# Two scan layers on one core: LayerNorm by tokens, the gate projection moved, one C product per state pair

## The chip, the cores and the metric

The kernel runs on 1 core of one Trainium2 chip. The metric is device microseconds of one execution; the verdict compares medians of several. The core has five engines with a queue each: PE (TensorE: matmuls, and PEld for their weight loads), DVE (VectorE), ACT (ScalarE), POOL (GpSimd) and SP (SyncE, which only issues DMAs here). An engine does its instructions in program order and waits on semaphores for the others.

## The reference

Two layers of a visual state-space model on `x` [8, 64, 64, 192], float32, each preceded by a normalization over groups of 6 channels and added to its input. One layer, cut to what is computed (K = 2 directions in layer 0, 4 in layer 1; 16 states; 384 inner channels; L = 64 x 64 = 4096 tokens):

```python
xz = jnp.einsum('bhwc,ec->bhwe', x, in_proj_w)          # 192 -> 768
xx, z = jnp.split(xz, 2, axis=-1)                       # 384 each; z is the gate
xc = silu(depthwise_conv_3x3(xx) + conv_b)
xs = ...                                                # the K orders of the 4096 tokens
dts, Bs, Cs = split(einsum('bkdl,kcd->bkcl', xs, x_proj_weight))
delta = softplus(einsum('bkrl,kdr->bkdl', dts, dt_projs_weight) + bias)
def step(h, inp):                                       # over the 4096 tokens
    dA = jnp.exp(dl_t[..., None] * As[None])
    h = dA * h + (dl_t * u_t)[..., None] * B_t[:, :, None, :]
    y = jnp.einsum('bkdn,bkn->bkd', h, C_t)             # the C product and the sum over states
y = sum over directions of (ys + xs * Ds), each put back in row order
y = (y - mean(y)) * rsqrt(var(y) + 1e-5) * ln_w + ln_b  # over the 384 channels of a token
y = y * gelu(z)                                         # silu(z) in layer 1
out = einsum('bhwd,od->bhwo', y, out_proj_w)            # 384 -> 192
```

## The kernel before

Channels lie on the 128 partitions (three tiles `dt` for 384 channels), tokens along the free axis, in chunks of T = 512 tokens, 8 chunks an image. A layer (`vss_layer`) has two stages, one after the other.

**The convolution stage** (`front`) goes over the 8 images in pairs of chunks, 32 pairs. `project` multiplies the normalized input by the first half of the input projection (PE into `pi`) and copies the result into a padded image `pad`. Of the nine taps of the 3 x 3 convolution, `first` does tap 0 on ACT, `second` taps 1 to NV-1 on DVE into `tp`, and `conv` the others on PE, as products with small diagonal blocks (`block_diag`, L151, 32 x 32 each, four at a time side by side); it adds `tp` through `mask` and applies Silu. NV is 5 in layer 0 and 4 in layer 1. The result goes to DRAM, as it is (`xcd`), turned to tokens on partitions (`turn`, `xtd`) and, in layer 1, by image columns (`columns`). `order` writes the order of all this out by hand.

**The scan stage** (`scans`) has a step for each image, direction and chunk: 128 steps in layer 0, 256 in layer 1. A step has 24 slots: 8 pairs of states (`m`) times 3 channel tiles (`dt`). The work of slot g:

- `scan` (L772): two `tensor_tensor_scan` on DVE, one for each state of the pair, h = da * h + hb over 512 tokens; then the product hc = h * C on POOL (L773), 2 x 512 elements a partition, with `cr` a row of C spread over the partitions.
- what `todo` holds for this slot, sorted by `rank_of`.
- `inject` for slot g + 2 (L728): 8 matmuls that put (delta * u) * B into `hb` (two PSUM buffers of two banks).
- `decay` for slot g + 4 (L745): two Exp on ACT into `da` (five buffers).

`at(i, s, f)` puts f into slot s of step i; the tables `L0_SLOTS` and `L1_SLOTS` hold these slots, and slots past 23 run on into the next steps. `reduce` adds hc of a state pair into `py` on PE (24 `block_diag` matmuls, L151), `load_c` loads the next `cr` from the SP queue, `dt_proj`, `dt_bias`, `softplus`, `turn_delta` (L683) and `make_dut` (L691) prepare the next step, `enter` (L665) and `carry` hand the state on. All matmuls of a step other than `hb` and `py` go through one PSUM bank, the tag `m`.

From the last direction of an image on, each finished chunk also goes through the LayerNorm work, functions with f_, spread over 2 steps in layer 0 and 4 in layer 1; the chunks of the last image take one step each (`L0_LAST`, `L1_LAST`), the very last one what remains. In order: `f_norm` normalizes the layer's input again (ACT), `f_gate` projects it to z (PE, 6 matmuls, L871) and `f_keep` copies it out (ACT); `f_sum`, `f_keep_sum` and `f_all` make each token's mean over the partitions by matmuls (L896, L911; `f_mean`, L888, in the last image); `f_center` subtracts it (DVE, L914); `f_square` (ACT), the same sums again, `f_rstd` (Ln and Exp, ACT), `f_scale` (DVE, L925); `f_act` is Gelu or Silu of z (ACT, L930), `f_affine` (ACT, L935), `f_times` (POOL, L944), `f_out` (PE, L950), `f_add` (DVE, L959), `f_store`.

Of the kernel before, what the change touches and what calls it, by code (L numbers as in the profile page):

```python
# [16 lines left out]
B = 8  # L17
# [33 lines left out]
    "turn_b": 3,  # L51
    "keep_b": 4,
    "dt_proj": (7, 0, 4),
    "dt_bias": (8, 2, 5),
    "turn_delta": (12, 15, 14),
    "make_dut": (13, 17, 15),
    "softplus": 10,
    "reduce": (5, 5),
    "add_y": 12,
    "add_turned": 26,  # L60
    "keep_y": 29,
    "f_norm": 8,
    "f_gate": ((9, 10), (18, 18), (22, 22)),
    "f_keep": (11, 20, 23),
    "f_sum": (20, 30),
    "f_keep_sum": (22, 31),
    "f_all": (23, 32),
    "f_center": 24,
    "f_square": 24,
    "f_rstd": 33,  # L70
    "f_scale": 33,
    "f_act": 34,
    "f_affine": (36, 35, 34),
    "f_times": (38, 39, 36),
    "f_out": ((42, 42, 42), (44, 46, 46)),
    "f_add": (43, 47),
# [3 lines left out]
    "load": 6,  # L80
    "f_norm": 8,
    "f_gate": ((10, 10), (11, 11), (9, 9)),
    "f_keep": (11, 12, 10),
    "f_act": 18,
    "f_mean": ((13, 13, 13), (18, 18, 18)),
    "f_center": 14,
    "f_square": 16,
    "f_rstd": 19,
    "f_scale": 19,
    "f_affine": (19, 20, 20),  # L90
    "f_times": (19, 20, 20),
    "f_out": ((21, 22, 22), (26, 26, 26)),
    "f_add": (23, 27),
# [4 lines left out]
    "turn_b": 6,  # L98
    "keep_b": 8,
    "dt_proj": (5, 8, 10),  # L100
    "dt_bias": (6, 10, 11),
    "turn_delta": (14, 15, 13),
    "make_dut": (15, 16, 14),
    "softplus": 11,
    "reduce": (5, 6),
    "add_y": 13,
    "add_turned": 24,
    "keep_y": 29,
    "f_norm": 6,
    "f_gate": ((11, 12), (17, 18), (20, 22)),  # L110
    "f_keep": (13, 19, 24),
    "f_sum": (41, 67),
    "f_keep_sum": (43, 70),
    "f_all": (45, 70),
    "f_center": 48,
    "f_square": 48,
    "f_rstd": 72,
    "f_scale": 72,
    "f_act": 59,
    "f_affine": (72, 76, 72),  # L120
    "f_times": (76, 79, 72),
    "f_out": ((83, 84, 84), (89, 91, 94)),
    "f_add": (85, 95),
}
L1_LAST = {
    "load": 6,
    "f_norm": 18,
    "f_gate": ((20, 20), (19, 19), (21, 21)),
    "f_keep": (21, 20, 22),
    "f_act": 22,  # L130
    "f_mean": ((11, 12, 12), (16, 16, 16)),
    "f_center": 13,
    "f_square": 16,
    "f_rstd": 17,
    "f_scale": 18,
    "f_affine": (19, 19, 19),
    "f_times": (22, 22, 22),
    "f_out": ((24, 24, 24), (28, 28, 28)),
    "f_add": (25, 29),
}  # L140
# [20 lines left out]
def load_weights(tc, ctx, name, w, K, rank, R, mask):  # L161
# [10 lines left out]
    get("w_in", [CP, CT, D], w["in_proj"][:, D:].rearrange("(t p) e -> p t e", p=CP))  # L172
# [27 lines left out]
    t["gnb"] = wp.tile([P, B, 2 + CT], F32, name="gnb")  # L200
    t["grs"] = wp.tile([P, B, 2 + CT], F32, name="grs")
# [3 lines left out]
def front(tc, name, x_src, xcd, xcd_col, xtd, xdd, w_in, t, clear, consts):  # L205
# [4 lines left out]
    ident, mask, grp, mean_w, all_w, eps_gn, eps_ln = consts  # L210
    cw, cb = t["cw"], t["cb"]

    NV = 4 if xdd is None else 5
    NH = NCH // 2
    with tc.tile_pool(name=f"{name}_a1", bufs=1) as a1, tc.tile_pool(
# [3 lines left out]
        w_x1 = a1.tile([P, D], F32, name="w_x1")  # L219
        nc.sync.dma_start(out=w_x1, in_=w_in[:P])  # L220
        w_x2 = a1.tile([P, D], F32, name="w_x2")
# [34 lines left out]
        def spread(im, w, src):  # L256

            for o in range(2 + CT):
# [15 lines left out]
        def group_means(b):  # L274
            im = ims[b]
            im["pg"] = psa.tile([P, 2, 2 + CT], F32, name="pg")
            spread(im, 0, im["mv"][:, :, 0])

        def deviations(b):
            im = ims[b]  # L280
            mv = im["mv"]
            gm = im["gm"] = a2.tile([P, 2 + CT], F32, name="gm")
            nc.vector.tensor_copy(gm, im["pg"][:, 0])
            dv = im["dv"] = a2.tile([P, 2], F32, name="dv")
            nc.vector.tensor_sub(dv, mv[:, :, 0], gm[:, :2])
# [3 lines left out]
        def variances(b):  # L289
            im = ims[b]  # L290
            spread(im, 1, im["dv"])
            gsd = a2.tile([P, 2 + CT], F32, name="gsd")
# [23 lines left out]
        def project(b, p, dt):  # L316
# [3 lines left out]
            cols = slice(dt * P, (dt + 1) * P)  # L320
# [4 lines left out]
            for r in range(2):  # L325
# [8 lines left out]
                )  # L334
            for r in range(2):
                c = 2 * p + r
                copy = nc.scalar.copy if dt == 2 and xdd is not None else nc.vector.tensor_copy
# [3 lines left out]
                )  # L341

# [72 lines left out]
        def order():  # L415
# [7 lines left out]
            for dt in range(DT):  # L423
                project(0, 0, dt)
                first(0, 0, dt)
                second(0, 0, dt)
            first(0, 1, *range(DT))
            second(0, 1, 0)
            normalize(0, 1, 2, 3)
            if B > 1:  # L430
                load(1, 0, 1)
# [5 lines left out]
            for g in range(B * NH):  # L437
# [3 lines left out]
                go = g + 1 < B * NH  # L441
                conv(b, 2 * p)
                for dt in range(DT):
                    if go:
                        project(n, q, dt)
                    if prev:
                        turn(*prev, dt)
                    if go:
                        first(n, 2 * q, dt)
                    if prev and xcd_col is not None:  # L450
                        columns(prev[0], prev[1] // 2, dt)
                    if p == 2 and more and dt == 1:
                        group_means(b + 1)
                if p == 0 and more:
                    load(b + 1, 2, 3)
                second(b, 2 * p + 1, 1, 2)
# [747 lines left out]
```

## Time and profile before

| | us |
|---|---|
| median of 3 runs | 25216.62 (25214.65 to 25219.68) |
| span of the profiled execution | 25231.1 |
| first scan of layer 0, last of layer 1 begin | 961.3, 25182.1 |
| busy in the span: PE, PEld | 24024.7, 13528.4 |
| busy in the span: DVE, ACT, POOL | 23345.8, 19452.6, 22144.2 |

One execution is profiled, and its own span is what sums are made against. In the profile, a line of a group gives the line of the kernel, the engine, the operation, the tiles written and read, their shapes and the number of instructions; then the time that the group kept its engine busy, the mean length of one in ns, and the idle time of the engine just before its instructions with what ended it. Instructions that follow one another overlap, so busy time by number is less than the mean length. PE's records count each float32 matmul twice, each transpose once. 0 to 961 us is the convolution stage of layer 0, then its scans to some 8930, the convolution stage of layer 1 to some 9865, and its scans to the end. The chain of work that ended last lies by 50% on PE, 25% on DVE and 19% on ACT:

```profile
PE 50%; DVE 25%; ACT 19%; issue 5%; DMA 1%; POOL 0%; SPq 0%; DVEq 0%; ACTq 0%; POOLq 0%
DVE h L772 22%; PE hb L728 20%; PE py L151 14%; ACT da L745 8%; PE pt L616 3%; PE pd L568 2%; PE pc L151 2%; PE po L950 2%; PE pz L871 2%; ACT delta L144 2%; ACT L144 1%; ACT L640 1%; PE pi L322 1%; ACT da L753 1%; ACT delta L630 1%
```

### The profile page before, as it was taken

Reading aid. Unit: us, or ns where it says so; the run is one execution under the profiler, and the core shown is the slowest. Engines: PE = TensorE matmul, PEld = TensorE weight load, DVE = VectorE, ACT = ScalarE, POOL = GpSimd, SP = SyncE. Lnnn points to the kernel's source line nnn. Section 1 sums busy time; section 2 is a strip of 40 time slices with the busy share of each in tenths; the row PEclk is TensorE's granted clock in tenths of the full one; section 3 lists DMA queues with packets and bytes.
Section 4 is the critical chain, followed back from the end, with each engine's and each line's share of the span. In section 5 each row is a group of like instructions: output and inputs, shape, how many; then the busy total and the mean of one; then the engine's idle time right before and its main releaser. Section 6 shows DMA issues by size and latency. Waiting matters only on the chain.

```text
span 25231.1 us, 794569 instructions
## 1 busy us (share of the span) xinstructions
PE 24024.7 (95%) x340032; PEld 13528.4 (54%) x340032; DVE 23345.8 (93%) x22142; ACT 19452.6 (77%) x37140; POOL 22144.2 (88%) x10287
## 2 busy tenths in 40 slices
PE   9999999999999999999999999999999999999999
PEld 4555555555555544555555555555555555555554
DVE  7899999999999777999999999999999999999998
ACT  5677788778878767777777777777777777777777
POOL 0499999999999713999999999999999999999998
PEclk9999999999999999999999999999999999999999
DMA  4566666666666555675675575675675575576575
GB/s 161 154 158 158 158 158 159 156 158 159 160 158 159 138 179 195 170 164 168 170 166 168 170 165 169 169 165 169 170 163 170 170 164 169 170 163 171 167 166 143
DMA packets 3836413, 4141.15 MB, mean 164 GB/s; under 512 B 2140460, under 2 KB 2340804, under 8 KB 3829828
## 3 DMA queue, kind: packets, MB, share of 16 engines
q1 hardware_dynamic: 3821296, 4032.72, 61.7%
q8 instruction: 2693, 44.12, 0.8%
q10 hardware_dynamic: 11604, 57.59, 0.6%
q14 instruction: 820, 6.72, 0.1%
HBM read 3443.63 MB, written 645.99 MB: 162 GB/s over the span
## 4 chain that ended last, share of the span: by engine, by line
PE 50%; DVE 25%; ACT 19%; issue 5%; DMA 1%; POOL 0%; SPq 0%; DVEq 0%; ACTq 0%; POOLq 0%
DVE h L772 22%; PE hb L728 20%; PE py L151 14%; ACT da L745 8%; PE pt L616 3%; PE pd L568 2%; PE pc L151 2%; PE po L950 2%; PE pz L871 2%; ACT delta L144 2%; ACT L144 1%; ACT L640 1%; PE pi L322 1%; ACT da L753 1%; ACT delta L630 1%
## 5 line engine op out<-in xcount | busy, mean ns | idle before, releaser
L773 POOL TENSOR_TENSOR hc<-h,cr 128x1024 f32<-128x1024 f32 x9216 | 21566.7, 2368 | 2985.7 <-DMA xt_k<-xtd 1844.7
L772 DVE TENSOR_TENSOR_SCAN h<-da,hb 128x512 f32<-128x512 f32 x18432 | 20860.2, 1199 | 1262.2 <-PE hb L728 1038.8
L745 ACT ACTIVATE da<-delta,a_neg 128x512 f32<-128x512 f32 x18432 | 12249.7, 713 | 1763.7 <-DVE h L772 1736.3
L728 PEld LDWEIGHTS hb<-dg,dut 64*128 64x128 f32 x147456 | 9215.4, 185 | 6720.3 <-issue 5785.3
L728 PE MATMUL hb<-dg,dut 64*128 64x128 f32 x147456 | 10835.6, 286 | 603.9 <-DVE h L772 413.0
L151 PE MATMUL py<-hc,mask 32*32 32x512 f32 x147456 | 6866.8, 601 | 36.0 <-ACT y L821 32.7
L151 PEld LDWEIGHTS py<-hc,mask 32*32 32x32 f32 x147456 | 1582.8, 103 | 2359.7 <-issue 1722.2
L753 ACT COPY da<-a 128x2 f32<-128x2 f32 x8064 | 1562.5, 194 | 293.9 <-ACT da L745 1.8
L778 ACT COPY st<-h 128x6 f32<-128x6 f32 x2688 | 537.4, 200 | 1142.3 <-DVE h L772 1140.0
L616 PE MATMUL pt<-xdbl,w_dt 96*128 96x512 f32 (+1 forms) x2304 | 1302.2, 646 | 38.8 <-DVE yc L914 15.9
L630 ACT ACTIVATE delta<-pt,dtb 128x512 f32<-128x512 f32 x1152 | 787.2, 683 | 449.5 <-PE pt L616 444.4
L355 DVE SCALAR_TENSOR_TENSOR tp<-pad,cw,tp 128x512 f32<-128x512 f32 x1344 | 988.2, 750 | 113.0 <-ACT tp L349 78.9
L683 PE MATMUL pq<-ident,delta 128*128 128x128 f32 x4608 | 758.7, 287 | 324.4 <-DVE dut L691 226.6
L871 PE MATMUL pz<-xn_sq,w_in 96*128 96x512 f32 x1536 | 835.3, 643 | 42.0 <-ACT g L882 27.2
L691 DVE TENSOR_TENSOR dut<-pq,xt_k 128x512 f32<-128x512 f32 x1152 | 767.7, 666 | 83.4 <-PE pq L683 83.4
L568 PE MATMUL pd<-x_k,w_x 128*128 128x512 f32 x1536 | 798.3, 629 | 35.8 <-DVE yc L914 15.1
L950 PE MATMUL po<-yc,w_out 128*96 128x512 f32 x1536 | 783.0, 621 | 16.2 <-POOL yc L944 13.3
L683 PEld LDWEIGHTS pq<-ident,delta 128*128 128x128 f32 x4608 | 484.2, 141 | 522.0 <-DVE dut L691 342.9
L151 PE MATMUL pc<-pad,taps 32*32 32x512 f32 x13824 | 577.9, 592 | 17.1 <-ACT xo L370 13.4
L821 ACT COPY y<-py 128x1536 f32<-128x1536 f32 x384 | 551.7, 1437 | 35.7 <-PE py L151 19.4
L144 ACT ACTIVATE delta<-delta 128x1536 f32<-128x1536 f32 x384 | 570.4, 1485 | 4.3
L944 POOL TENSOR_TENSOR yc<-yc,g 128x512 f32<-128x512 f32 x384 | 490.0, 1279 | 79.1 <-ACT yc L935 72.9
(105 smaller groups left out, 10143.1 us busy)
## 6 DMA issues: line engine op xcount, KB each, us to landing
cr<-cscr SPq DMA_DIRECT2D x2048, 512.0 KB, 4.4
dg<-dgd SPq DMA_DIRECT2D x1536, 512.0 KB, 7.9
cr<-xdd SPq DMA_DIRECT2D x1024, 512.0 KB, 6.4
xt_k<-xtd SPq DMA_DIRECT2D x768, 384.0 KB, 7.1
xcd<-xo SPq DMA_DIRECT2D x128, 768.0 KB, 3.5
xtd<-xv SPq DMA_DIRECT2D x128, 768.0 KB, 4.4
y<-yrow SPq DMA_DIRECT2D x128, 768.0 KB, 5.0
yc<-yrow SPq DMA_DIRECT2D x128, 768.0 KB, 7.2
```

Source lines behind the costliest of these rows:

```text
L144: nc.scalar.activation(out, in_, AF.Softplus)
L151: nc.tensor.matmul(out[j * Q : (j + 1) * Q, dt], w[i * Q : (i + 1) * Q], x[i * Q : (i + 1) * Q], start=first, stop=last, tile_position=(i ...
L568: nc.tensor.matmul(live[i]["pd"][:R], w_x[:, dt, k, :], live[i]["x"][:, dt], start=(dt == 0), stop=(dt == DT - 1),)
L616: nc.tensor.matmul(pt, w_dt[:, k, dt * P : (dt + 1) * P], live[i]["xdbl"][:rank], start=True, stop=True,)
L683: nc.tensor.transpose(pq[:, g], live[i]["delta"][:, dt, g * P : (g + 1) * P], ident)
L728: nc.tensor.matmul(hv[:, r, q], live[i]["dut"][r * G : (r + 1) * G, dt, q], dg[r * G : (r + 1) * G, q, :, 2 * mm : 2 * mm + 2], start=True ...
L745: nc.scalar.activation(da[:, n].rearrange("p (r g j) -> p r g j", r=2, j=G), live[i]["delta"][:, dt].rearrange("p (g r j) -> p r g j", r=2 ...
L753: nc.scalar.copy(da[:, :, f], live[i]["a0"][:, dt, 2 * m : 2 * m + 2])
L772: nc.vector.tensor_tensor_scan(o, a, v, init, ALU.mult, ALU.add)
L773: nc.gpsimd.tensor_mul(hc[:, dt], h[:, dt], live[i]["cr", m])
L871: nc.tensor.matmul(fin["pz"], w_in[:, u, dt * P : (dt + 1) * P], fin["xn"][:, u], start=(u == 0), stop=(u == CT - 1),)
L950: nc.tensor.matmul(fin["po"][:CP], w_out[:, dt, u * CP : (u + 1) * CP], fin["y"][:, dt], start=(dt == 0), stop=(dt == DT - 1),)
```

## The change

Three parts, with new slot tables for all of the scan stage's work.

- The gate projection moves into the convolution stage: `gates` multiplies the same input by the second half of the projection (whose channels stand in the order of the scans), applies Silu in layer 1 (Gelu of layer 0 stays where it was, `f_act`) and stores `zd` in DRAM, from where `f_load_g` fetches it. `f_norm`, `f_gate` and `f_keep` go.
- Taps 1 to NV-1 on DVE become more: NV is 8 in layer 0 and 7 in layer 1. `second` goes over taps and, within each, over the three tiles, and `order` is rewritten.
- LayerNorm works on tokens: `f_turn` transposes 128 tokens x 384 channels through PSUM (PE), and then mean, square sum and scaling are per partition, on ACT, with sums taken by the instructions themselves (`accum_out`); `f_back` transposes back, and `f_affine` reads that from PSUM. Only a 128 x 4 product (`f_rstd`) is DVE's.
- `scan` issues one POOL product for a state pair, after its third tile, with C broadcast over the tiles; `h` has three buffers. The slot of `reduce` moves from 5, 5 to 7, 7 in layer 0 and from 5, 6 to 6, 7 in layer 1.

```diff
-    "reduce": (5, 5),
-    "add_y": 12,
+    "reduce": (7, 7),
+    "add_y": 15,
...
+    "load": (16, 14, 7),
+    "f_act": 39,
+    "f_turn": (18, 20, 21, 22),
+    "f_take": (19, 21, 22, 23),
+    "f_mean": 23,
+    "f_square": (23, 25, 24, 25),
+    "f_rstd": 27,
+    "f_scale": (28, 31, 30, 30),
+    "f_back": (33, 35, 36),
+    "f_affine": (34, 36, 37),
+    "f_times": (39, 39, 39),
...
-    NV = 4 if xdd is None else 5
+    NV = 7 if xdd is None else 8
...
+        def gates(b, p, dt):
+
+            pi = product(b, p, DT + dt)
+            zo = a2.tile([P, 2, T], F32, name="zo")
+            for r in range(2):
+                if gate is None:
+                    nc.scalar.copy(zo[:, r], pi[r])
+                else:
+                    nc.scalar.activation(zo[:, r], pi[r], gate)
+            nc.sync.dma_start(
+                out=zd[b][dt * P : (dt + 1) * P, 2 * p * T : 2 * (p + 1) * T],
+                in_=zo.rearrange("p r l -> p (r l)"),
+            )
...
-        def second(b, c, *dts):
-            for dt in dts:
-                tv = ims[b]["tp", c][:, dt].rearrange("p (h w) -> p h w", w=W)
-                for s in range(1, NV):
+        def second(b, c, *taps):
+            for s in taps:
+                for dt in range(DT) if s < NV else ():
+                    tv = ims[b]["tp", c][:, dt].rearrange("p (h w) -> p h w", w=W)
...
-                    s2.tile([P, DT, 2, T], F32, name="h"),
+                    s2.tile([P, DT, 2, T], F32, name="h", bufs=3),
                     s2.tile([P, DT, 2, T], F32, name="hc", bufs=3),
...
-            nc.gpsimd.tensor_mul(hc[:, dt], h[:, dt], live[i]["cr", m])
+            if dt == DT - 1:
+                cr = live[i]["cr", m].unsqueeze(1).to_broadcast([P, DT, 2, T])
+                nc.gpsimd.tensor_mul(hc, h, cr)
...
+        def f_load_g(v, b, c):
+            sl = slice(c * T, (c + 1) * T)
+            v["g"] = s1.tile([P, DT, T], F32, name="g")
+            nc.sync.dma_start(out=v["g"], in_=tiles(zd[b])[:, :, sl])
+
+        def f_turn(v, q):
+
+            v["pu", q] = psy.tile([P, D], F32, name="pu", tag="m")
+            for dt in range(DT):
+                nc.tensor.transpose(
+                    v["pu", q][:, dt * P : (dt + 1) * P],
+                    v["y"][:, dt, q * P : (q + 1) * P],
+                    ident,
+                )
...
             nc.scalar.activation(
+                v["yt"][:, q], v["pu", q], AF.Identity, accum_out=v["sum"][:, q : q + 1]
+            )
+
+        def f_mean(v):
+            nc.scalar.mul(v["sum"], v["sum"], -1.0 / D)
...
+            nc.scalar.activation(
+                v["sq"],
+                v["yt"][:, q],
+                AF.Square,
+                bias=v["sum"][:, q : q + 1],
+                accum_out=v["ssq"][:, q : q + 1],
+            )
+
+        def f_rstd(v):
+            ssq = v["ssq"]
+            nc.scalar.activation(ssq, ssq, AF.Ln, bias=eps_ln, scale=1.0 / D)
+            nc.scalar.activation(ssq, ssq, AF.Exp, scale=-0.5)
+            nc.vector.tensor_mul(v["sum"], v["sum"], ssq)
+
+        def f_scale(v, q):
+            nc.scalar.activation(
+                v["yt"][:, q],
+                v["yt"][:, q],
+                AF.Identity,
+                bias=v["sum"][:, q : q + 1],
+                scale=v["ssq"][:, q : q + 1],
+            )
+
+        def f_back(v, dt):
+            v["pb", dt] = psy.tile([P, T], F32, name="pb", tag="m")
+            for q in range(T // P):
+                nc.tensor.transpose(
+                    v["pb", dt][:, q * P : (q + 1) * P],
+                    v["yt"][:, q, dt * P : (dt + 1) * P],
+                    ident,
+                )
```

`place` puts these into slots for every chunk, with the tables `L0_LAST` and `L1_LAST` for the last image and new ones, `L0_ENDS` and `L1_ENDS`, for its last chunk. The `f_rstd` slot of layer 1 is 53, of layer 0 it is 27.

More of the change, by code (lines that the diff above doesn't have):

```diff
@@ L461, in order @@
                 if go:
-                    second(n, 2 * q, *range(DT))
-                if more and (p, 0) in sets:
-                    stats(b + 1, *sets[p, 0])
-                conv(b, 2 * p + 1)
-                for dt in range(DT):
-                    turn(b, 2 * p, dt)
-                if xdd is not None:
-                    x_proj(b, 2 * p)
+                    gates(n, q, 0)
+                    gates(n, q, 1)
                 if p == 2 and more:
-                    variances(b + 1)
                     normalize(b + 1, 0)
@@ L476, in order @@
                     normalize(b, p + 2)
+                conv(b, 2 * p + 1)
+                if go:
+                    gates(n, q, 2)
+                    second(n, 2 * q, *range(1, 9))
+                for dt in range(DT):
+                    turn(b, 2 * p, dt)
+                if xdd is not None:
+                    x_proj(b, 2 * p)
                 if go:
                     first(n, 2 * q + 1, *range(DT))
-                    second(n, 2 * q + 1, 0)
-                if more and (p, 1) in sets:
-                    stats(b + 1, *sets[p, 1])
+                if xcd_col is not None:
+                    for dt in range(DT):
+                        columns(b, p, dt)
+                for e in range(2):
+                    if more and (p, e) in sets:
+                        stats(b + 1, *sets[p, e])
                 if p == 1 and more:
@@ L1065, in scans @@
+                place(e, slots, b, c)
+        for c in range(NCH):
+            place(N - NCH + c + 1, ends if c == NCH - 1 else last, B - 1, c)
         rank_of = {
```

460 lines of the change are left out of this document (190 added, 270 removed).

## The prediction

> **What bounds the kernel now.** I read the busy time by stage first (columns: stretch, its length, then PE, PEld, DVE, ACT and POOL busy with instruction counts, granted clock, DMA share, GB/s). The four stretches are the convolution stage of layer 0, its scans, the convolution stage of layer 1, its scans.
>
> ```profile
> 200.00:800.00 600.00, 592.80 (x6606) 286.75 (x6611) 483.49 (x724) 332.51 (x549) 0.00 (x0) 1.00 0.46 159
> 6000.00:7000.00 1000.00, 955.06 (x13693) 566.79 (x13674) 952.74 (x868) 807.89 (x1546) 953.17 (x446) 1.00 0.66 159
> 9000.00:9500.00 500.00, 481.21 (x6630) 239.19 (x6638) 372.39 (x575) 362.62 (x522) 0.00 (x0) 1.00 0.55 198
> 18000.00:19000.00 1000.00, 961.68 (x13784) 533.03 (x13786) 945.05 (x865) 782.67 (x1525) 952.49 (x440) 1.00 0.69 167
> ```
>
> The convolution stages are PE's (99% and 96%), with DVE at 81% and 74% and POOL idle. In the scans PE, DVE and POOL all stand at 95%: no one engine alone is the bound. The groups of lines of 14000 to 18000 us (layer 1, 3218 scans / 48 = 67.0 steps, so 59.7 us a step) give the prices; idle before each group and its releaser stand last:
>
> ```profile
> L772 DVE TENSOR_TENSOR_SCAN h<-da,hb 128x512 f32<-128x512 f32 x3218 | 3636.3, 1199 | 186.5 <-PE hb L728 152.7 <-ACT st L778 22.7 <-ACT da L753 6.8
> L773 POOL TENSOR_TENSOR hc<-h,cr 128x1024 f32<-128x1024 f32 x1610 | 3768.5, 2370 | 152.9 <-DVE h L772 147.8 <-DMA cr<-cscr 2.9
> L944 POOL TENSOR_TENSOR yc<-yc,g 128x512 f32<-128x512 f32 x51 | 65.3, 1280 | 1.0
> L871 PE MATMUL pz<-xn_sq,w_in 96*128 96x512 f32 x192 | 108.0, 645 | 0.0
> L683 PE MATMUL pq<-ident,delta 128*128 128x128 f32 x804 | 131.8, 287 | 65.8 <-DVE dut L691 41.6 <-ACT g L882 24.1
> ```
>
> DVE waits for hb from PE, POOL waits for h from DVE, and PE waits in turn for DVE to free a hb buffer. Which of the three closes the ring shows in single steps of layer 1: one without any LayerNorm work, one with the gate projection, one with the gate product and output projection.
>
> ```profile
> 10319.30:10376.20 56.90, 53.38 (x832) 31.01 (x820) 55.60 (x53) 41.28 (x71) 56.22 (x26) 1.00 0.59 169
> 11778.70:11839.70 61.00, 58.26 (x832) 32.18 (x829) 55.96 (x52) 47.32 (x96) 56.20 (x27) 1.00 0.66 187
> 11954.90:12016.50 61.60, 59.97 (x848) 32.85 (x838) 58.63 (x55) 48.63 (x99) 60.60 (x30) 1.00 0.55 154
> ```
>
> The empty step is POOL's: 24 x 2.37 = 56.9. Six gate matmuls with 96 rows of w_in, nothing else new, make it 61.0 (PE). Three products on POOL, 3 x 1.28 = 3.84, and the output projection make 61.6 (POOL and PE). The steps between, with L914 and L925 on DVE, take 57.4 and 57.8. So the change's removals fall on what sets the end.
>
> [...]
>
> **The change, part by part.**
>
> *Scan stage, per chunk of LayerNorm (64 a layer; one every 2 steps in layer 0, every 4 in layer 1, one a step in the last 7 steps of each).* PE loses pz, 108.0/16 = 6.75 us, and ps and pm, 2.1 + 2.25; it gains 12 + 12 transposes at 131.8/804 = 0.164, so 3.9. Net -7.2 (layer 0 by its own rows -6.6). DVE loses L914 and L925, 1.73 each, and keeps two adds of 0.66. ACT loses two normalizations, three copies, two sums, the square and the pair Ln/Exp over 512, some 9 us, and gains 12 passes over 384 elements, 0.5 to 0.6 each, with small ones, some 7.5; it is busy 78% and sets no end; in layer 1 the gate's activation, 1.48, and its table load, 1.28, leave it too. SP gains one load of 768 KB; the same size from yrow lands in 7.2 us and is issued 11 slots or more ahead. The one PSUM bank m, for which PE waits until ACT or DVE has emptied it (65.7 us of these 4000 at pq), changes hands nine times a chunk before (pz 3, ps 2, pm 2, po 2) and after (pu 4, pb 3, po 2): no term.
>
> *One C product in place of three (L773).* Per element (2.37 - 1.28)/512 = 2.13 ns, fixed 0.19; 3072 elements make 6.73 (between 6.54, no fixed part, and 7.11, nothing saved). Eight a step: 53.8 for 56.9, so POOL leaves the bound, 53.8 + 0.5 (L665) + 3.84 per chunk being at most 56.2 a step. The price: it starts only after the third scan and ends 6.73 later, and the reduction's matmuls, PE's queue behind them and cr's next load on SP (already waiting for hc 1944.7 us of these 4000) wait for it. Three scans take 6.8 to 7.05, reductions move from slots 5, 5 to 7, 7 (layer 0) and from 5, 6 to 6, 7 (layer 1). PE reaches slot 3m+6 after scan 3m+5 and one injection of 1.19, so 6.8 + 1.2 = 8.0 after the product could start: slack 1.3 in layer 1, 3.6 in layer 0. cr then lands 4.4 to 6.4 after, some 13 of 21 available. I take this at nothing; what covers it is that slack.
>
> *A 128x4 product on DVE (f_rstd).* Nothing like it, two SBUF operands while POOL works, is in the trace: every DVE product there in the scans has an operand in PSUM. Lower bound: the 128x2 products of the convolution stage, 0.16. Upper bound: it is held as long as a whole hc product runs, 6.7, with the scans queued behind it on DVE and PE and POOL behind these. It is nearest to the first row; I take 1.0 for its wait for ACT's Exp too, 128 x 1.0 = +128, bounds +20 and +860.
>
> [...]
>
> *Scan time.* DVE's floor a step: 48 x 3636.3/3218 = 54.24, dut 3 x 0.666 = 2.0, so 56.24, and 1.5 a chunk. Now a step takes 61.4 in layer 0 (1432.5 to 8307.5 us, 112 steps, by each step's first scan) and 59.7 in layer 1 (11244.3 to 24622.7, 224 steps); DVE is idle 213.6/65 = 3.3 and 186.5/67 = 2.8 of it. With PE relieved and POOL off the bound I leave half: 1.7 and 1.4. Layer 0, per chunk: 2 x 56.24 + 1.5 + 3.4 = 117.4 for 122.8, -5.4 x 56 = -302. Layer 1: 4 x 56.24 + 1.5 + 5.6 = 232.1 for 238.9, -6.8 x 56 = -381. The last 7 steps a layer (81.5 and 72.9 now, DVE waiting for hb 70.9 of the last 500 us) lose 8 of PE and some DVE work each: -9 x 14 = -126. Together -809, bounds -450 (idle stays; only DVE's 3.3 per chunk and the last steps) and -1150 (idle of 0.5 a step).
>
> *Convolution stage, per pair of chunks (32 a layer).* Three taps go from PE to DVE, and the gates' matmuls come in. Layer 0: PE loses 3 x 1.02 x 2 = 6.1 (4126 tap records, 174.6 us), gains a second projection, 5.84 + 3.39 = 9.2: 27.7 now, some 30. DVE has 7 x 3 x 2 = 42 taps at 381.3/517 = 0.74, 31.0, with statistics 1.9 and small ones 0.4: 33.3. ACT: 332.5/21.5 = 15.5 plus 3 pad copies and 6 gate copies at 0.55: some 21. DVE becomes the bound; 3% idle gives 34.0, +6.2. Layer 1: DVE 36 x 0.733 = 26.4, three pad copies 1.9, statistics 1.9, small 0.4: 30.6 for PE's 26.3 now; PE 27.5, ACT 25.6; 31.5, +5.2. The order of taps by s, then tile, puts independent taps after one another; statistics, independent too, overlap by 0.057 each, and by that DVE would be 2 less. Store zd: 6 x 512 KB x 0.5 a pair on 46% and 55% busy DMA, hidden. Sum 32 x 11.4 = +365, +10 for the first chunk; bounds +250 and +560 (DVE 85% busy).
>
> *Sum* against the profiled execution: 25231 - 809 + 375 + 128 = 24925. The median of the runs is 14 lower, so 24910.
>
> **Rivals.** *DVE at its floor* (chance 0.18): idle falls to 0.5 a step, -1150 + 375 + 100: some 24550. For it: in the empty steps DVE already works 55.60 of 56.90. Against: two hb buffers and bursts of 24 reductions remain.
>
> *The convolution stages take it back* (0.16): idle stays, -450 + 375 + 128: 25270 in the profile, 25050 to 25330 as a range. For it: layer 0 still issues both reductions in one slot, and its steps without LayerNorm work take 57.7 to 58.4 already.
>
> *Slower: PE waits for the long product* (0.16). Place: the reductions' matmuls on hc (L151), then hb, then the scan, each of 3072 times. Where a product ends after its slack, the excess stalls DVE; 0.35 us each makes +1075, so 25231 - 306 + 1075 = 26000. It decides from 306/3072 = 0.10 us on. For it: POOL falls back by 3.84 in a chunk of layer 0, past the 3.6. Against: it makes up about 0.3 a product, and PE has room between injections.
>
> *The stages overlap otherwise than I think* (0.04), a DMA late for instance, either side.
>
> **How the numbers follow.** The forecast, 24910 with an own range of 24700 to 25100, has 0.46. About 0.2% (50 us) is what a measurement can tell from no change. Faster: 0.46 + 0.18 + 0.05 of the second rival + 0.02 = 0.71; same 0.07; slower 0.16 + 0.04 + 0.02 = 0.22. The range, 24540 to 25330, holds the forecast, the floor and the second rival; it leaves out the long wait.
>
> **What would show it.** hc at 128x3072 near 6.7 us, POOL below 94% in the scans; steps of 58.0 in layer 1 and 58.7 in layer 0; DVE the busiest engine of the convolution stages, pairs of 34 and 31.5 us; the 128x4 product without a long idle time before it or length of its own. Wrong would be: hc above 7.1; idle PE before L151's matmuls waiting for hc; convolution pairs above 37; DVE standing at the 128x4 product.

## The result, and the profile after

The changed kernel takes 26723.92 us (median of 4 runs, 26714.13 to 26745.65), the kernel before beside it 25218.15 (25214.65 to 25233.91): a ratio of 1.0597 (1.0582 to 1.0612), so it is slower. The profiled spans are 26720.3 and 25231.1 us, 1489 apart, where the prediction had 306 less.

Busy time by stage of the changed kernel (columns as before: stretch, length, PE, PEld, DVE, ACT, POOL with counts, granted clock, DMA share, GB/s), for the convolution stage and scans of layer 0, then of layer 1:

```profile
200.00:800.00 600.00, 567.49 (x3393) 233.28 (x3392) 553.46 (x876) 377.84 (x656) 0.00 (x0) 0.97 0.51 185
6000.00:7000.00 1000.00, 867.63 (x12466) 536.95 (x12459) 874.52 (x788) 754.90 (x1503) 839.02 (x170) 0.95 0.60 151
10000.00:10500.00 500.00, 435.05 (x3268) 177.63 (x3271) 412.67 (x649) 355.15 (x548) 0.00 (x0) 0.92 0.58 217
18000.00:19000.00 1000.00, 935.59 (x13781) 535.17 (x13775) 928.04 (x857) 772.54 (x1555) 911.50 (x174) 0.99 0.64 171
```

No engine stands at 95% any more: in layer 0's scans all four (PE, DVE, ACT, POOL) have fallen to 75 to 87%, and PE's granted clock from 1.00 to 0.95. Lost time is waiting. Four groups of the page, over the whole run:

```profile
L820 POOL TENSOR_TENSOR hc<-h,cr 128x3072 f32<-128x3072 f32 x3072 | 20664.6, 6736 | 5358.3 <-DVE h L817 2581.6
L817 DVE TENSOR_TENSOR_SCAN h<-da,hb 128x512 f32<-128x512 f32 x18432 | 20819.3, 1199 | 2400.8 <-PE hb L773 1946.3
L176 PE MATMUL py<-y,mask 32*32 32x512 f32 x6144 | 501.1, 722 | 355.2 <-DMA y<-ycol 355.1
L897 PE MATMUL pu<-ident,yc 128*128 128x128 f32 x1536 | 307.9, 314 | 416.2 <-DMA yc<-yrow 392.9
```

Of the kernel before, the scans over the whole run, the sums of y at 14000 to 18000 us and the first matmuls that read yc at 2000 to 6000 us:

```profile
L772 DVE TENSOR_TENSOR_SCAN h<-da,hb 128x512 f32<-128x512 f32 x18432 | 20860.2, 1199 | 1262.2 <-PE hb L728 1038.8
L151 PE MATMUL py<-y,mask 32*32 32x512 f32 x1176 | 76.0, 758 | 0.0
L896 PE MATMUL ps<-yc,mean_w 128*32 128x512 f32 x198 | 35.0, 605 | 0.0
```

The long C product takes 6736 ns as estimated, and the scans wait for hb from PE, as before, but nearly twice as long (1946.3 us for 1038.8). New are two waits of PE itself for a DMA: 392.9 us for yc, at the first transpose of the LayerNorm work, and 355.1 for y from ycol, the sums of the turned directions. Steps by each step's first scan, and stages between them, place the 1489 us:

| us | before | after | difference | predicted |
|---|---|---|---|---|
| convolution stage, layer 0 (to the first scan) | 961.3 | 1106.7 | +145 | +208 |
| layer 0, 9 steps without LayerNorm work, each | 58.8 | 59.9 | +10 in all | 0 |
| layer 0, 112 steps with it, each | 61.4 | 66.6 | +575 | -302 + 56 |
| layer 0, last 7 steps | 557.1 | 571.0 | +14 | -63 + 8 |
| convolution stage, layer 1 | 937.5 | 1182.9 | +245 | +167 |
| layer 1, third direction, 64 steps, each | 60.4 | 68.3 | +511 | part of -381 + 56 |
| layer 1, other steps with it, 167, each | 59.4 | 58.4 | -175 | the rest of it |
| layer 1, last 8 steps and end | 608.4 | 770.8 | +162 | -63 + 8 |

The 17 steps of layer 1 that are not listed, without LayerNorm work, take 57.0 us in both kernels. Of the 64 steps of the third direction 56 have LayerNorm work; these go from 60.6 to 68.6 us, and the figures for this direction below are of them.

### The profile page after: what moved, and what is told of

It reads as the page before. It is cut to its first block, busy times and chain, and to the rows that moved or that the text cites. A ratio compares the mean times of both kernels' runs of the same rounds, so it can differ in the third digit from the quotient of the medians.

```text
span 26720.3 us, 774945 instructions
## 1 busy us (share of the span) xinstructions
PE 23913.3 (89%) x331648; PEld 13682.6 (51%) x331648; DVE 23681.5 (89%) x22922; ACT 19860.2 (74%) x39367; POOL 21258.1 (80%) x4143
## 5 line engine op out<-in xcount | busy, mean ns | idle before, releaser
L820 POOL TENSOR_TENSOR hc<-h,cr 128x3072 f32<-128x3072 f32 x3072 | 20664.6, 6736 | 5358.3 <-DVE h L817 2581.6
L817 DVE TENSOR_TENSOR_SCAN h<-da,hb 128x512 f32<-128x512 f32 x18432 | 20819.3, 1199 | 2400.8 <-PE hb L773 1946.3
L773 PEld LDWEIGHTS hb<-dg,dut 64*128 64x128 f32 x147456 | 9402.6, 189 | 7084.1 <-issue 6069.9
L773 PE MATMUL hb<-dg,dut 64*128 64x128 f32 x147456 | 11044.8, 290 | 1244.0 <-DVE h L817 1225.8
L176 PE MATMUL py<-hc,mask 32*32 32x512 f32 x147456 | 6973.9, 611 | 1.9 <-issue 1.9
L398 DVE SCALAR_TENSOR_TENSOR tp<-pad,cw,tp 128x512 f32<-128x512 f32 x2496 | 1665.7, 745 | 83.8 <-ACT tp L392 82.6
L346 PE MATMUL pi<-x,w_x 128*128 128x512 f32 x1536 | 782.2, 632 | 48.2 <-ACT xv L437 22.3
L176 PE MATMUL py<-y,mask 32*32 32x512 f32 x6144 | 501.1, 722 | 355.2 <-DMA y<-ycol 355.1
L908 ACT ACTIVATE xn_sq<-pu 128x384 f32<-128x384 f32 x512 | 248.9, 486 | 629.2 <-PE pu L897 628.4
L897 PE MATMUL pu<-ident,yc 128*128 128x128 f32 x1536 | 307.9, 314 | 416.2 <-DMA yc<-yrow 392.9
```

The costliest lines, as they stand in the source:

```text
L176: nc.tensor.matmul(out[j * Q : (j + 1) * Q, dt], w[i * Q : (i + 1) * Q], x[i * Q : (i + 1) * Q], start=first, stop=last, tile_position=(i ...
L346: nc.tensor.matmul(pi[r], w_x1[:, cols], part_of(im, 2 * p + r), start=True, stop=False)
L398: nc.vector.scalar_tensor_tensor(tv, window(dt, c, s), cw[:, dt, s : s + 1], tv, ALU.mult, ALU.add)
L773: nc.tensor.matmul(hv[:, r, q], live[i]["dut"][r * G : (r + 1) * G, dt, q], dg[r * G : (r + 1) * G, q, :, 2 * mm : 2 * mm + 2], start=True ...
L817: nc.vector.tensor_tensor_scan(o, a, v, init, ALU.mult, ALU.add)
L820: nc.gpsimd.tensor_mul(hc, h, cr)
```

## The experiments

Each kernel was measured once, with the kernel before beside it (25206.6 to 25246.3 us); a difference in whole time below these 40 us carries nothing. By stage the runs tell more than by their whole time.

**Five buffers for cr** (run cr5). SP, which issues DMAs in order, stands at the next cr until a buffer comes free (3835.3 us over layer 0's steps with LayerNorm work, 203.3 over eight steps of layer 1's third direction, 13697 to 14246); in layer 0 yc's fetch is behind it.

```diff
-            cr = s2.tile([P, 2, T], F32, name="cr", bufs=3)
+            cr = s2.tile([P, 2, T], F32, name="cr", bufs=5)
```

> The changed kernel with five buffers for cr instead of three, so that SP no longer waits for the long product before each C row. Theory A (the long C product frees cr's buffers later, SP stands there in order, and what is queued behind it, yc in layer 0 and the twelve turned loads of y in layer 1, reaches PE too late): layer 0's steps with LayerNorm work fall from 66.3 us to 59 to 61, the steps of the third direction of layer 1 from 68.6 to about 60, some -1000 us together, 25650 us. Theory B (the product itself is too long, PE waits for hc): nothing changes, 26720. Theory C (the loads are simply put into slots too late for their landing time, whatever SP does): the two waits of PE shrink by less than half, 26400 or more.

26370.2 us. Layer 1's third direction falls from 68.6 to 63.2. Layer 0's steps with LayerNorm work stay at 66.4, but not because nothing happened: SP issues yc some four slots sooner, and PE's wait for it goes from 279.0 us to 1.6. So the queue did help to make yc late, though SP's standing at cr is not new (3831.6 us over these steps in the kernel before); what is new is yc's place behind it. In the place of this wait SP now stands at the next xt_k until dut is made (1952.6 us over these steps for 238.6), and PE stands at reductions (95.9 us for none) and at injections (59.7 for 3.1) for something that the profile does not show; DVE's wait for hb rises from 553 to 708. One wait was exchanged for others.

**yc fetched earlier in layer 0** (yc_early).

```diff
-    "load": (16, 14, 7),
+    "load": (16, 8, 7),
```

> The changed kernel with the load of yc in layer 0 in slot 8 instead of 14; the turn that reads it stays in slot 18. Theories A and C: PE's 279 us of waiting for yc in layer 0's scans go, with what follows from them (PE's clock drops, hb late): 280 to 600 us less, 26100 to 26440; layer 1 unchanged. If the steps of layer 0 are long for another cause (the 128x4 product, the transposes in the one PSUM bank, the long C product), less than 100 us.

26455.6 us, 267 less by the spans; layer 0's steps fall from 66.6 to 64.0, -287. Waits of the changed kernel, then of this run, over the layer 0 steps (engine, line, what it waited for: us in total, times, longest):

```profile
ACT xn_sq L908 <- PE pu L897: 486.8, 126, 6.8
...
PE pu L897 <- DMA yc<-yrow: 279.0, 56, 6.2
DVE h L817 <- ACT da L798: 273.5, 144, 5.5
```

```profile
ACT xn_sq L908 <- PE pu L897: 196.8, 126, 3.7
...
PEld pu L897 <- DVE dut L736: 92.3, 56, 1.7
...
PE pu L897 <- DVE dut L736: 80.9, 56, 1.5
...
DVE h L817 <- ACT da L798: 36.1, 80, 1.8
```

Each of 56 chunks made PE stand 5 us for yc, ACT behind PE at L908, and DVE behind ACT, which had not yet made da: three engines in a row. With the fetch six slots earlier PE's wait for the DMA is gone, and DVE's for da falls from 273.5 to 36.1 us.

**The 128x4 product on ACT** (sum_act).

```diff
-            nc.vector.tensor_mul(v["sum"], v["sum"], ssq)
+            for q in range(T // P):
+                nc.scalar.activation(
+                    v["sum"][:, q : q + 1], v["sum"][:, q : q + 1], AF.Identity, scale=ssq[:, q : q + 1]
+                )
```

> The changed kernel with the 128x4 product of f_rstd on ACT as four activations with a scale per partition, instead of on DVE. If DVE is held there by POOL's product: its 186 us in layer 0's scans and some 44 us in the last image of layer 1 leave DVE, and the time falls by 150 to 250 us, 26470 to 26570. If these lengths lie in time that DVE would have waited anyway: within 50 us of 26720.

26515.7 us, layer 0's steps at 64.7 (-1.9 each, -212), the last 8 steps of layer 1 -34; with what other stages lost the whole is 206 less by the spans. The DVE group of the changed kernel over the layer 0 steps (busy, mean ns):

```profile
L930 DVE TENSOR_TENSOR f_sum<-f_sum,f_ssq 128x4 f32<-128x4 f32 x55 | 185.6, 3375 | 0.0
```

Four elements a partition take 3375 ns on the mean. Over the whole run the shortest was 135 ns and the longest 6518, just short of a whole hc product; in layer 1's 56 chunks before the last image it took 137 on the mean. The trace shows what holds it: in all 56 steady chunks of layer 0 a POOL product was running when it began, and it ended 15 to 24 ns after that product; in none of the 56 of layer 1 was one running.

**Turned sums added later in layer 1** (add26).

```diff
-    "add_turned": 22,
+    "add_turned": 26,
```

> The changed kernel with the sum of the turned y (layer 1, third direction of each image, 64 steps) in slot 26 instead of 22. If PE's wait for the last of the twelve loads makes these steps 68.6 us: they fall to 59 to 61, some -500 us, 26200. If they are long for another cause: within 100 us of 26720.

26293.4 us: the third direction's steps fall from 68.6 to 61.4. Waits over layer 1's steps, of the changed kernel and of this run:

```profile
PE py L176 <- DMA y<-ycol: 355.1, 66, 11.3
```

```profile
PE py L176 <- DMA y<-ycol: 35.4, 14, 3.5
```

The twelve fetches of a turned chunk lie at slots 8 to 19 in both kernels; the change had moved their use from 24 to 22.

**The edits together, and four gate buffers** (combo).

```diff
-            zo = a2.tile([P, 2, T], F32, name="zo")
+            zo = a2.tile([P, 2, T], F32, name="zo", bufs=4)
```

> The changed kernel with the three single edits together (yc fetched at slot 8 in layer 0, the 128x4 product on ACT, the turned sums added at slot 26 in layer 1) and, new, four buffers instead of two for zo, the gate tile of the convolution stage. Theory A (three separate late waits, each with its own stretch of slow PE clock): the gains add, -287, -212 - 35 and -430, so some 25750 before zo; layer 0's steps with LayerNorm work at 62.1 us (66.6 now). Rival B (the waits hide one another, a step has one last wait): layer 0's steps stay near 64.0, the whole near 25950. For zo apart, by the convolution stage of layer 1 (1182.9 us now): if ACT standing 12 us for a gate buffer once an image is what makes its pairs 34.8 us, it falls by 7 x (12 to 20) = 85 to 140, to some 1070, and the whole to 25640; if the store is only the last of several late transfers there, it stays above 1150.

25614.4 us: the three gains add, as A has it, and layer 0's steps come to 62.0. The convolution stages fall by 46 and 68 us, in layer 1 less than the 85 to 140 expected. Waits in layer 1's convolution stage of the changed kernel, and of combo:

```profile
ACT zo L380 <- DMA zd<-zo: 71.2, 7, 12.0
...
PE px L436 <- ACT zo L380: 60.9, 7, 10.6
```

```profile
ACT zo L380 <- PE pi L351: 92.9, 61, 3.0
```

Once an image ACT stood 10 us on the mean, 12 at most, for a gate tile whose store was late, with PE behind it. That is gone. The stage then has PE at 89% and DVE at 85% (9150 to 10200 us), for 84% and 79% in the changed kernel (9700 to 10840); what still holds it was not followed up.

**More cr buffers on top** (combo_cr5: cr with five, and in the last image of layer 1 `"load": (13, 7, 12)` for `(12, 9, 6)`).

> The kernel of the run combo, with five buffers for cr instead of three and, in the last image of layer 1, yc fetched at slot 7 (9 before), g at 12 (6) and x at 13 (12). Theory: fetches queued on SP behind a load that waits for a cr buffer still come late in layer 1's third direction, so its steps go from about 61.4 to 60 or less (56 x 1.5 = -85), and the last image's stretch falls by 5 us a chunk, 670 to 635. Rival: with the sums at slot 26 nobody waits for these fetches any more, the steps stay within 0.5 us of combo's; and the last stretch is set by the chain of ACT passes, within 10 us of combo's.

25870.9 us, worse: the third direction gains 1.4 us a step and the last image 24, but layer 0's steps rise from 62.0 to 65.1. It is the exchange of cr5 again: SP stands at the next xt_k until dut is made (2105.2 us over these steps for 4.7), PE at injections (121.4 us for 7.8) and reductions (95.5 for 0.6) for something that the profile does not show, and DVE's wait for hb rises from 479 to 737. What PE waits for there stays open.

**Three C products again** (combo_three).

```diff
-            if dt == DT - 1:
-                cr = live[i]["cr", m].unsqueeze(1).to_broadcast([P, DT, 2, T])
-                nc.gpsimd.tensor_mul(hc, h, cr)
+            nc.gpsimd.tensor_mul(hc[:, dt], h[:, dt], live[i]["cr", m])
```

> The kernel of the run combo, with the C product undone: three POOL products of 128x1024 for each pair of states (2.37 us each), all else alike. Theory 1 (the prediction's: one long product costs nothing where the reductions are moved to 7, 7 and 6, 7, and takes POOL off the bound): POOL has 56.9 + 3.84 a chunk, so layer 0's steps with LayerNorm work cannot go below 58.8 and the empty steps of layer 1 stay at 56.9; the whole within 0.3% of combo or slower. Rival (the long product holds PE's reductions up and costs more than POOL's relief gives): layer 0's steps fall by 1 us or more against combo, layer 1's by 0.5 or more, the whole by 200 us or more.

25506.0 us, 108 less than combo. Neither theory holds as put: layer 0's steps are the same (62.25 for 62.04), the third direction and the last 7 steps of layer 0 gain 72 and 38. So POOL's relief bought nothing, and the long product cost little: 108 us.

**One C product alone, and its companion** (before_c1, before_r77). Both start from the kernel before, in layer 0 only; the first also has the long product and three h buffers.

```diff
-    "reduce": (5, 5),
-    "add_y": 12,
+    "reduce": (7, 7),
+    "add_y": 15,
...
-    "keep_y": 29,
+    "keep_y": 30,
```

> The kernel before with one part of the change alone, in layer 0 only: one C product of 128x3072 for each pair of states, three buffers for h, reductions at slots 7, 7, sums at 15, keep_y at 30. Theory (prediction's term: nothing to pay, POOL from 56.9 to 53.8 a step): steps with LayerNorm work 61.4 or up to 0.5 less, the whole 25170 to 25260. Rival (PE waits for the long product): 0.35 us for each of 24 injections a step, so 8 us a step and layer 0 longer by 1000; half of it already shows as steps above 63. Second rival, from the pairs of state buffers: reductions and sums bunch behind the product at the step's end, 1 to 2 us a step, +110 to +220.

> The kernel before with the reductions of layer 0 at slots 7, 7, the sums at 15 and keep_y at 30, and three C products as they were: the companion of before_c1, which has the one long product besides and steps of 64.5 us without LayerNorm work and 68.9 with it (58.8 and 61.4 before). Theory A (the long product itself holds PE up): here the steps stay at 58.8 and 61.4 within 0.5 us. Theory B (the later reductions collide with the slots of before, the product is innocent): here the steps are 64 and 68 as in before_c1. Between them, each has its share by where the steps fall.

26174.3 and 26150.0 us against 25246.3 and 25234.5; steps with LayerNorm work 68.9 and 69.1, without it 64.5 and 64.1. The later reductions alone cost 7.7 us a step among the other slots of before, and the long product adds nothing to these steps; only the last 7 of layer 0 are longer with it (597 us for 567). Alone, before_c1 would have been read as proof against the product; its companion takes that reading away.

**Layer 0's own slots as before, and the last image of layer 1** (base_l0, from combo_three; it also fetches yc at slot 6 in layer 0, and yc at 8 and g at 12 in the last image).

```diff
-    "turn_delta": (17, 19, 15),
-    "make_dut": (18, 20, 16),
-    "softplus": 13,
-    "reduce": (7, 7),
+    "turn_delta": (12, 15, 14),
+    "make_dut": (13, 17, 15),
+    "softplus": 10,
+    "reduce": (5, 5),
...
-    "f_out": ((24, 24, 24), (28, 28, 28)),
-    "f_add": (25, 29),
+    "f_out": ((28, 28, 28), (31, 31, 31)),
+    "f_add": (29, 32),
```

> The kernel of the run combo_three, with two edits in places that do not meet. In layer 0 the slots of all the work that a step has without LayerNorm are those of the kernel before (reductions at 5, 5, dt_proj, softplus, turn_delta, make_dut, keep_y), and yc is fetched at slot 6. In the last image of layer 1 the output projection has slots 28 and 31 for 24 and 28, yc is fetched at 8, g at 12. Theory for layer 0: its steps without LayerNorm work are 60.1 us in combo_three and 58.8 before, and only these slots differ; so they return to 58.8, and the steps with LayerNorm work from 62.2 to 61 or less, which then is what LayerNorm by tokens is worth against 61.4 (112 x 1.2 = -135). Rival: the slots of before meet the new transposes in the one PSUM bank m, and the steps with LayerNorm work stay at 62 or rise, though the others fall. For the last image of layer 1: if PE stands there for the product with g on POOL (41.6 + 35.4 us at the output projection in combo), the stretch falls from 661.7 by 40 us or more; if the chain of passes is what is long, it stays within 15 us.

25528.9 us. The last 8 steps of layer 1, up to the last scan, fall from 661.7 in combo_three to 587.8, as the theory has it: PE stood there for the products with g on POOL. Waits of combo's last image, and of this run's:

```profile
PEld po L972 <- POOL yc L966: 34.7, 10, 6.4
...
PE po L972 <- POOL yc L966: 29.5, 5, 6.2
```

```profile
PEld po L970 <- issue: 12.0, 45, 0.3
...
PEld po L970 <- ACT bt L650: 2.0, 5, 0.4
```

PE's wait for these products was 20.0 us in combo_three and is gone, but its wait for yc fell as well, from 39.2 to 16.0, by the other edit; how much of the 74 us each gave stays open. In layer 0 the rival came true: steps without LayerNorm work return to 58.2, those with it rise to 63.0, now as 58.5 and 67.6 in turn.

**Four more runs on layer 0's long step.** best1 (from base_l0) moves the transposes back from slots 33, 35, 36 to 33, 34, 35, with small moves in layer 0's last image; best1_dve (from best1) puts the 128x4 product back on DVE; best2_gelu (from best1) does so in layer 0 alone and moves layer 0's Gelu (f_act) from slot 39 to 15; best2 (from best2_gelu) moves the transposes and squares to `"f_turn": (11, 18, 19, 20)`, `"f_square": (21, 22, 23, 24)`, with f_rstd at 25 and f_scale from 27.

> The kernel of the run base_l0 (three C products, layer 0's own slots as before) with f_back of layer 0 at slots 33, 34, 35 for 33, 35, 36, away from turn_delta, which stands in the same slot 12 of the next step and uses the same PSUM bank; in the last image of layer 0 the last transpose is at 13 and the second output projection at 26. In base_l0 the second step of each chunk is 67.6 us, the first 57.8, and in such a long step PE stands at pb for dut and DVE 4.5 us for da. Theory: this one collision makes the second step long; it falls to 61 or less, the mean step with LayerNorm work to 59.5 (63.0 in base_l0, 61.4 before), -390, and with 25 from the last image the whole comes to some 25110, below the kernel before. Rival: the chain of ACT passes of the second step (rstd, scale, affine) makes ACT late with da whatever the slots of f_back; then the second step stays above 65 and the whole above 25400.

> The kernel of the run best1 with the 128x4 product of f_rstd back on DVE (128x128 such products, as in the changed kernel, where it took 3.4 us on the mean in layer 0 and up to 6.5, 0.137 when nothing held it). Theory (it is held as long as the POOL product that runs at its side): with POOL products of 2.37 us it takes 2.4 us at most and about 1.2 on the mean, and layer 0's steps rise by at most 0.6 against best1. Rival (its length has another cause, ACT's results or a fixed cost): it keeps its 3.4 us on the mean, with single ones above 5.

> The kernel of the run best1 with layer 0's Gelu of the gate (f_act) at slot 15 instead of 39, that is in the first step of a chunk instead of the second, and the 128x4 product on DVE in layer 0 alone. In best1 the second step of a chunk is 66 to 68 us, the first 57.5 to 59; ACT works without a gap through the first third of the second step and again around its table loads (Gelu 1.49 with 2 x 1.28 for its tables), and the scans wait for da and hb behind it. Theory (ACT's bursts in the second step set layer 0's steps): 4.05 us of ACT move to the step that has room; the second step falls by 2 to 4 us, the first rises by less than 1, the mean from 62.5 to 61.5 or less (-110). Rival (ACT only follows DVE there): the second step stays at 66 to 68.

> The kernel of the run best2_gelu with layer 0's first half of the LayerNorm chain earlier and farther apart: transposes at slots 11, 18, 19, 20, the squares at 21 to 24, rstd at 25, the scaling at 27, 28, 30, 31; yc is still fetched at 6. Theory (ACT's bursts): the squares leave the second step's first slots, its stretch without a gap ends some 3 us earlier, the mean step with LayerNorm work comes to 60.5 or less and the whole to 25250 or less, the kernel before's own time. Rival (the chain is too long for two steps however it is laid; the burst moves into the first step): the mean stays within 0.7 us of best2_gelu's.

25474.6, 25483.1, 25633.3 and 25519.8 us; steps with LayerNorm work 62.7, 62.3, 64.1 and 63.1. best1's collision was not the cause. best1_dve bears out the theory of the held product, whose mean fell with the POOL product from 3375 to 607 ns:

```profile
L928 DVE TENSOR_TENSOR f_sum<-f_sum,f_ssq 128x4 f32<-128x4 f32 x55 | 33.4, 607 | 0.0
```

The theory of ACT's bursts falls: with 4 us of ACT moved away the second step became longer (69.4 us for 66.3 in best1_dve). (Steps without LayerNorm work differ by 0.8 us among these runs though no edit of theirs touches them; less than that in layer 0 carries nothing.) PE's waits in best1 at 2000 to 8000 us show what is left (the second line is 121.6 to 155.6 in the other three):

```profile
PE hb L773 <- DVE h L817: 219.4, 381, 1.3
PE pb L945 <- ACT yc L955: 141.2, 69, 3.2
```

PE stands at the transposes back until ACT has emptied the one bank m. Slots clear both of one another and of dut (base_l0's wait there, 105.4 us) were not tried, so whether that is the cause of their long steps stays open; combo, which hardly has this wait (2.3 us), has steps of 62.0 all the same.

best1, the fastest of these, is at 25474.6, 0.98% above the kernel before on the same chip (25227.9): it recovers 1248 of the 1489 us and beats the changed kernel, not the kernel before. Of the 241 us that are left, the convolution stages have 98 and 172 and layer 0's steps with LayerNorm work 145; the last 8 steps of layer 1 have 35; layer 1's other steps give back 167 and 28, layer 0's last steps 21, and small ones make up the rest.

## Why the prediction was wrong

**The step that failed** is the one on SP and the loads: "SP gains one load of 768 KB; the same size from yrow lands in 7.2 us and is issued 11 slots or more ahead." That is true of the gate's load at slot 7. But yc's own fetch moved from slot 6 to 14, and its use from the sum at 20 to a transpose at 18: 4 slots, 11 us, where there had been 14 slots. PE, which stands in order, uses it first in both kernels. And 7.2 us was too short a landing: in layer 0's steps with LayerNorm work yc landed 12.3 us after its issue on the median, 7.1 in the kernel before. I costed the load that was added and not the load that was moved. The same holds for add_turned, from 24 to 22 in the slot table, of which the prediction says nothing. By stage the two are 287 us in layer 0's steps (yc_early) and 464 in the 64 steps of the third direction (add26); by whole time 267 and 429.

**The scan term**, "-809, bounds -450 and -1150", fails with it, and also by itself. "With PE relieved and POOL off the bound I leave half" of DVE's idle time: it did not halve anywhere. In layer 1 no fetch is late in 167 steps, and these fell by 1.05 us each, where 1.7 was put. Sixteen of them before and twenty-four after (columns as above):

```profile
11717.00:12668.00 951.00, 918.31 (x13304) 511.57 (x13280) 910.49 (x833) 751.73 (x1464) 917.93 (x425) 1.00 0.60 169
12299.00:13697.00 1398.00, 1327.35 (x19886) 764.82 (x19882) 1340.94 (x1240) 1119.41 (x2257) 1310.42 (x249) 1.00 0.63 175
```

A step goes from 59.4 to 58.3 us, DVE's work in it from 56.9 to 55.9, its idle time from 2.5 to 2.4, though PE's work fell by 2.1 us and POOL's by 2.8. So the gain is the work taken off DVE, and for layer 1 the bound of the prediction under which "idle stays" is the one that holds; what keeps the idle time was not followed up. In layer 0 DVE's idle time rose from 3.3 to 8.3 us a step, and with the late waits mended (combo) it is still 5.4; DVE's work fell there from 58.2 to 56.6, but the steps stay above the 61.4 of before, for a cause that is not settled.

**PE's clock** was taken as full. It is 0.963 over the span for 0.995. Windows of the changed kernel around one wait for yc, and PE's timeline there (start, length, instruction, idle time before it):

```profile
2756.00:2760.00 4.00, 3.03 (x43) 2.41 (x36) 4.00 (x5) 2.38 (x6) 3.56 (x3) 1.00 1.07 226
2760.00:2765.00 5.00, 0.03 (x1) 0.06 (x1) 2.68 (x3) 0.00 (x0) 4.54 (x1) 0.82 0.97 296
2765.00:2768.00 3.00, 3.00 (x20) 2.45 (x21) 0.03 (x1) 2.09 (x6) 0.00 (x0) 0.50 0.80 155
2768.00:2771.00 3.00, 3.00 (x50) 1.30 (x51) 2.88 (x3) 1.54 (x4) 0.47 (x1) 0.67 0.28 87
2771.00:2774.00 3.00, 3.00 (x52) 2.17 (x35) 1.12 (x1) 0.75 (x3) 3.00 (x1) 1.00 0.50 119
```

```profile
2757.83 1.20 PE L773 MATMUL hb<-dg,dut 64*128 64x128 f32 x16
2764.97 0.87 PE L897 MATMUL pu<-ident,yc 128*128 128x128 f32 x3 [5.94 <-DMA yc<-yrow]
2765.77 2.08 PE L773 MATMUL hb<-dg,dut 64*128 64x128 f32 x16
...
2771.53 1.20 PE L773 MATMUL hb<-dg,dut 64*128 64x128 f32 x16
```

PE stands 5.94 us; 4.1 us into that time its clock falls to 0.50, until 2770.0, and the injection that follows takes 2.08 us for 1.20. This wait cost more than its length, by 0.88 us for that injection alone. Over the span PE's idle stretches above 1.5 us went from 183 to 411, the time at half clock from 254 to 1957 us. Not every drop comes in so long a wait: 0.50 also begins at 2797.3, after an idle stretch of 2.33 us, and lasts until 2807.5. What sets its start, these runs do not show.

**The 128x4 product on DVE**, +128 with bounds +20 and +860: 246 by sum_act, in layer 0's steps and the last image of layer 1 (206 in the whole time). Inside the bounds, twice the size. The sum took 1.0 us for it, from the nearest row; it measured 3.4 on the mean in layer 0, where it ended 15 to 24 ns after the POOL product at its side, each of 56 times, as the upper bound had it (why, no run shows), and with three POOL products in place of the long one (best1_dve) the mean fell to 0.6. In layer 1's steady chunks, with no POOL product beside it, it cost nothing, 137 ns.

**One C product**: 6.73 us estimated, 6.736 measured; "at nothing" holds within 108 us. The gain from POOL's leaving the bound, which the scan term had leant on, did not come: POOL is below 94% as forecast, but with three products layer 0's steps are the same.

**Convolution stages**: +375 predicted, 145 + 245 = 390 measured. That it fits so well is partly luck, since two errors cancel. Layer 0's pair of chunks costs less than put, for taps overlap: 2496 of them keep DVE busy 1665.7 us in the whole run, 0.67 each where 0.74 was put; with the stall for zo mended DVE and PE stand at 98% and 99% there (300 to 900 us of combo). Layer 1's costs more; the store of zd was called hidden, and at two buffers it was not (ACT stood at zo for it 45.2 us in layer 0 and 71.2 in layer 1).

**The last images**, -126 predicted, +14 and, up to the last scan, +147 measured: PE's work was taken out, but the chain of transposes, passes and products lies in one step there, with a slot or so between stages, and in layer 1 PE waits in it for ACT, POOL and the yc fetch (55.2, 36.1 and 36.7 us) at a clock of 0.82.

**The rivals.** The slower one named PE's waits as its place, but for the long product; the waits were for DMAs. before_r77 and combo_three show the product is not it. The place was named by the rival with the smallest chance, 0.04: stages that overlap otherwise, "a DMA late for instance".

## What to carry to other kernels

When work is moved between slots, list for each load the slot that issues it and the slot that uses it, before and after; a moved user counts as much as an added load, and most when the user is an engine that others follow in their order, as PE was here (yc_early took away its 279.0 us of waits for yc, and ACT's behind it at L908 fell from 486.8 to 196.8). Busy time taken off an engine is worth only what the waits left in its step allow (in layer 1 2.1 us less of PE's work, 2.8 of POOL's and 1.0 of DVE's made a step 1.05 shorter), and a new wait on PE can be paid twice, as idle time and as slow clock after it (5.94 us idle, then an injection of 2.08 for 1.20). A buffer added for one load can move the queue's wait to the next load and cost as much (in cr5 PE's wait for yc fell from 279.0 us to 1.6, SP's wait at xt_k rose from 238.6 to 1952.6, and the steps stayed at 66.4 for 66.6). A part tried alone among slots set for other work needs a companion run that has its slots without the part.

## What was not expected of the hardware

A DVE product of 4 elements a partition took 135 to 6518 ns, and beside a POOL product in layer 0 it ended 15 to 24 ns after that one, each of 56 times. A PE idle stretch of 2.33 us was followed, 0.8 us after its end, by 10 us of half clock (2797.3 to 2807.5). More buffers for one load (cr5, combo_cr5) left layer 0's steps the same in one kernel (66.4 us for 66.6) and made them 3 us longer in another (65.1 for 62.0), though in the first they took away PE's wait for yc.
